# Layer 1's cross attention in a two-layer decoder: the value products turned round, and the softmax sums taken from the matrix unit to GpSimd and DRAM

## The chip, the cores and the metric

The kernel runs on one core of one Trainium2 chip. The core has five engines with queues of their own: TensorE (matrix products and transposes), VectorE, ScalarE, GpSimd and SyncE, which here only issues DMAs. The metric is the time of the whole program on the device in microseconds, as the median of several runs. In the profile the engines are called PE (matrix products), PEld (loading of the stationary operand), DVE (VectorE), ACT (ScalarE), POOL (GpSimd) and SP (SyncE); a trailing q marks an engine's queue, where DMAs are issued.

## The reference

Two decoder layers over x of 32 x 56 x 128, each with an attention over x or a recurrent mixer, a cross attention to a context of 32 x 1500 x 128, and a mixture of experts. All of it is fp32. The change touches only the cross attention of layer 1, which has 16 heads of 64:

```python
xn = _layernorm(x, ln_gamma, ln_beta)
q = (xn @ w_q).reshape(B, SQ, NUM_HEADS, DIM_HEAD)
k, v = jnp.split(context @ w_kv, 2, axis=-1)
k = k.reshape(B, SK, NUM_HEADS, DIM_HEAD)
v = v.reshape(B, SK, NUM_HEADS, DIM_HEAD)
scores = jnp.einsum('bqhd,bkhd->bhqk', q * SCALE, k)
attn = jax.nn.softmax(scores, axis=-1)
out = jnp.einsum('bhqk,bkhd->bqhd', attn, v).reshape(B, SQ, INNER)
out = (out @ w_out + b_out) * jnp.tanh(gate[0])
```

## The kernel before

The head matrices are folded at the start: key weights into the query projection (`m1`) and value weights into the output projection (`n1`). Each head's query then has 128 features and meets the raw context, so the attention of one batch element is 896 queries (16 heads x 56) against 1500 context rows of 128 features. Queries and, later, their results share the tiles `qo` (features on the partitions, queries along the row).

`attention()` takes the 896 queries of each of the 32 batch elements in two blocks of 512 and 384 (`BLOCKS`, line 66), 64 blocks in all. The 1500 context rows are 12 chunks of 125. For a block there are these steps:

- Scores (line 1088): 12 products, one a chunk, with a chunk of the transposed context `amT` stationary and the queries moving. The result has context rows on the partitions and queries along the row. ScalarE copies each from one of three PSUM banks (`p_s`) into the block's tile `s` (line 1089).
- Maxima: VectorE keeps a running elementwise maximum of the chunks in `m` (lines 1094 to 1098). TensorE transposes it, VectorE reduces it to the negative maximum of each query (`maxima`), and TensorE and ScalarE spread that over 125 partitions as `nb` (`spread`, line 1174).
- Probabilities (`probabilities`): in four parts of three chunks VectorE adds `nb` (line 1182) and ScalarE takes the exponential in place (line 1185).
- Values (`values`): for each 128 queries, 12 products with the probabilities stationary and the context rows `amN` moving, 129 columns wide; the last column of `amN` is one, so column 128 of the result is the sum of the probabilities. VectorE takes its reciprocal (line 1200), ScalarE scales by it into `ao` (line 1202).
- Outputs (`outputs`): TensorE transposes each `ao` (128 x 128) back, and VectorE copies the four or three of them into `qo` (line 1210).

The steps of three blocks are interleaved: while block i's scores are made, the rest of block i-1's probabilities (`tail`) and block i-2's outputs are done; then come block i-1's values, with block i's maxima and the first of its probabilities among them. The value results use two PSUM banks (`p_v`), the maxima's and outputs' transposes one (`p_t`), everything else two more (`p_f`).

Around this main thread run generators for everything that stands before layer 1's cross attention (`pre`, for four batch elements at a time) and behind it (`post`). Each `yield` of the attention is a place at which the loop at the end of `decoder_kernel` can let one of them go on; how far is decided by a planned time of TensorE (`clock["pe"]`), counted from the products issued, and by the constants `PRE_US`, `POST_US` and `PAIR_US`, the planned TensorE time of the attention of two batch elements. The framework's scheduler then fixes the order of instructions in each engine's queue. The layer norms take their inverse root on GpSimd (`root`, line 367, a power of one column), which is most of what GpSimd does. The big loads (`amT`, `amN`, expert weights) are issued from SP's queue.

Of the kernel before, what the change touches and what calls it, by code (L numbers as in the profile page):

```python
# [63 lines left out]
PRE_US, POST_US, PAIR_US = 71.3, 31.0, 80.5  # L64
# [5 lines left out]
def decoder_kernel(  # L70
# [88 lines left out]
    x_first = [const.tile([TP, D], F32, name=f"x_first{i}") for i in range(2)]  # L159
# [29 lines left out]

    qo = [const.tile([P, 2, NQ], F32, name=f"qo{i}") for i in range(3)]  # L190
# [878 lines left out]

    def attention():  # L1070
# [4 lines left out]
        for i in range(len(blocks) + 2):  # L1075
            cur = None
            if i < len(blocks):
# [8 lines left out]
                for c in range(CK):  # L1086
# [16 lines left out]
                    if c == 5 and old is not None:  # L1103
                        outputs(old)
                        old = None
# [4 lines left out]
            elif old is not None:  # L1110
                outputs(old)
                old = None
            for f in tail:
                f()
            tail = []
            os = []
            nt = prev[2] // P if prev else 0
            for t in range(max(nt, 2)):
                if t < nt:
                    po = values(prev, t)  # L1120
                    for k in range(3):
                        next(po)
                        if t == 1 and k == 1 and cur:
                            table["gelu"] = False
                            nb = spread(cur, nm)
                            tail = probabilities(cur, nb)
                            for f in tail[:1]:
                                f()
                            tail = tail[1:]
                        yield 0  # L1130
                    os.append(next(po))
                elif t == 1 and cur:
                    yield 1.0
                    nb = spread(cur, nm)
                    tail = probabilities(cur, nb)
                if t == 0 and cur:
                    if not nt:
                        yield 1.0
                    nm = maxima(cur, m)
                if t >= 2 and tail:  # L1140
                    tail.pop(0)()
            if prev:
                old = (prev, os)
# [45 lines left out]
    def values(blk, t):  # L1189
        b, _, _, s = blk  # L1190
        po = bank(p_v, "v")
        for c in range(CK):
            mm(
                po[:, : D + 1], s[:, c, t * P : (t + 1) * P], amN[b % 2][:, c, :],
                start=(c == 0), stop=(c == CK - 1),
            )
            if c % 4 == 3:
                yield
        rz = tiny.tile([P, 1], F32, tag="rz1", name="rz1")
        nc.vector.reciprocal(rz, po[:, D : D + 1])  # L1200
        o = work.tile([P, D], F32, tag="ao", name="ao", bufs=5)
        nc.scalar.activation(o, po[:, :D], AF.Copy, scale=rz)  # L1202
        yield o
# [203 lines left out]
```

## Time and profile before

| | |
|---|---|
| median of three runs | 2205.03 us (2204.17 to 2207.74) |
| the profiled execution, its own time | 2197.48 us |
| its span, first to last instruction | 2194.7 us |
| TensorE busy, granted clock | 2131.5 us (97%), 0.99 |
| VectorE busy | 1435.0 us (65%) |
| ScalarE busy | 1194.3 us (54%) |
| GpSimd busy | 143.8 us (7%) |
| DMA engines' mean share | 27.3% of 16 engines' time for the queue of the program's loads and stores |
| value products of layer 1 | 5376 instructions, 276 ns each from start to modelled end |
| scores of layer 1 | 768 instructions of 512 columns (594 ns) and 768 of 384 (493 ns) |
| transposes of `ao` | 224 instructions, 275 ns each |

A row of the profile reads: line, engine, operation, what is written and from what, the shapes, how many, and then times. Instructions of TensorE overlap, so a mean duration is longer than what one instruction adds; the start of one group and the start of the next tell what a group takes. An fp32 product appears as two instructions, a transpose as one. In the table of waits, the three numbers after a row are the total in us, how often, and the longest. In a timeline a row begins with the start and the length in us, and a bracket at its end gives the idle time in front of it and what ended that. A tile's own row gives the shortest, median and longest duration in ns.

### The profile page before, as it was taken

The page shows a single profiled execution, that of the slowest core. Times are in us where ns is not written, and L with a number is a line of the kernel's source. Part 1 is how long each engine was busy: PE and PEld are TensorE (multiplying, and loading weights), DVE is VectorE, ACT ScalarE, POOL GpSimd, SP SyncE. Part 2 cuts the span into 40 slices and gives each one's busy share as a digit, 9 for nine tenths or more (in the row PEclk, how much of TensorE's full clock was granted, in tenths as well). Part 3 has the DMA queues.
Part 4 walks back from the last instruction along what each step waited for, and adds up shares of the span by engine and source line. Part 5 has one row for each costly group of instructions (what it writes and reads, how often), then busy time and mean ns, then how long its engine had stood idle before and what let it go on. Part 6 is the DMA issues. An engine that isn't in the chain of part 4 may idle for free.

```text
span 2194.7 us, 36640 instructions
## 1 busy us (share of the span) xinstructions
PE 2131.5 (97%) x14496; PEld 1694.8 (77%) x14496; DVE 1435.0 (65%) x2961; ACT 1194.3 (54%) x2128; POOL 143.8 (7%) x230
## 2 busy tenths in 40 slices
PE   8899999999999999999999999999999999999997
PEld 5667787788777787777877788777887878778877
DVE  4377657765676756776577665777567765667774
ACT  3346655555654655555565656555555556465551
POOL 2010001000110001000010000100001000000000
PEclk8999999999999999999999999999999999999999
DMA  8503320153213432034311343113321132111221
GB/s 222 151 17 85 108 65 22 56 134 98 60 31 78 116 91 65 17 79 125 102 44 31 113 98 91 34 57 91 101 87 29 57 107 84 41 43 50 59 82 38
DMA packets 161996, 167.96 MB, mean 77 GB/s; under 512 B 9209, under 2 KB 136609, under 8 KB 161697
## 3 DMA queue, kind: packets, MB, share of 16 engines
q1 hardware_dynamic: 161568, 165.51, 27.3%
q8 instruction: 114, 1.87, 0.4%
q14 instruction: 58, 0.47, 0.1%
q10 hardware_dynamic: 256, 0.11, 0.0%
HBM read 140.09 MB, written 25.49 MB: 75 GB/s over the span
## 4 chain that ended last, share of the span: by engine, by line
PE 70%; DVE 9%; ACT 3%; POOL 2%; issue 1%; DMA 1%; POOLq 0%; DVEq 0%; ACTq 0%
PE f L146 25%; PE s L146 20%; PE v L146 19%; DVE s L1182 4%; PE f L155 3%; PE t L155 3%; POOL rs L367 2%; DVE m L1094 1%; ACT s L1185 1%; DVE m L1098 1%; ACT nb L1174 0%; DVE st L358 0%; DMA memT<-big 0%; DVE m L1096 0%; ACT s L1089 0%
## 5 line engine op out<-in xcount | busy, mean ns | idle before, releaser
L146 PE MATMUL v<-amN,s 125*128 125x129 f32 x5376 | 694.0, 276 | 0.0
L146 PEld LDWEIGHTS v<-amN,s 125*128 125x128 f32 x5376 | 655.0, 191 | 35.7 <-issue 23.3
L146 PE MATMUL s<-qo,amT 128*125 128x512 f32 (+1 forms) x1536 | 649.2, 543 | 1.6 <-ACT s L1089 1.5
L1089 ACT COPY s<-s 125x512 f32<-125x512 f32 (+1 forms) x768 | 399.7, 539 | 274.0 <-PE s L146 271.6
L1182 DVE TENSOR_TENSOR s<-s,nb 125x1536 f32<-125x1536 f32 (+1 forms) x256 | 393.0, 1547 | 61.2 <-ACT nb L1174 60.7
L146 PEld LDWEIGHTS s<-qo,amT 128*125 128x125 f32 x1536 | 263.4, 188 | 160.0 <-issue 95.3
L1185 ACT ACTIVATE s<-s 125x1536 f32<-125x1536 f32 (+1 forms) x256 | 339.5, 1330 | 86.4 <-DVE s L1182 81.0
L1094 DVE TENSOR_TENSOR m<-m,s 125x1024 f32<-125x1024 f32 (+1 forms) x192 | 209.1, 1089 | 67.3 <-ACT s L1089 64.7
L367 POOL TENSOR_TENSOR rs<-rs,mhalf 112x1 f32<-112x1 f32 x122 | 79.8, 664 | 1730.4 <-DVE rs L366 1559.0
L1202 ACT ACTIVATE ao<-v,rz 128x128 f32<-128x128 f32 x224 | 81.1, 363 | 164.4 <-DVE rz L1200 164.3
L772 ACT ACTIVATE hT<-f,vec 128x224 f32<-128x224 f32 x256 | 97.7, 447 | 89.8 <-PE f L146 89.5
L146 PEld LDWEIGHTS f<-wd,hT 128*112 128x112 f32 x1024 | 119.5, 177 | 19.2 <-ACT hT L772 8.8
L146 PE MATMUL f<-wd,hT 128*112 128x128 f32 x1024 | 128.8, 275 | 2.1 <-ACT hT L772 1.9
L146 PE MATMUL f<-pxT,w 128*128 128x224 f32 (+1 forms) x576 | 117.7, 344 | 2.5 <-DVE th L958 0.9
L146 PE MATMUL f<-xT,wu 128*128 128x224 f32 x512 | 114.7, 360 | 2.8 <-DMA wu<-in_wup_dram 2.7
L146 PEld LDWEIGHTS f<-pxT,w 128*128 128x128 f32 x576 | 99.0, 195 | 18.8 <-issue 3.5
L1094 DVE TENSOR_TENSOR m<-s 125x1024 f32<-125x1024 f32 x64 | 69.6, 1088 | 63.7 <-ACT s L1089 63.3
L146 PEld LDWEIGHTS f<-xT,wu 128*128 128x128 f32 x512 | 93.2, 192 | 19.9 <-issue 7.8
L790 DVE SCALAR_TENSOR_TENSOR acc<-f,wmix,acc 112x128 f32<-112x128 f32 x128 | 43.9, 348 | 88.8 <-PE f L146 88.7
L1098 DVE TENSOR_TENSOR m<-m,s 125x384 f32<-125x384 f32 (+1 forms) x128 | 80.4, 628 | 21.3 <-ACT s L1089 15.2
L1174 ACT COPY nb<-t 125x512 f32<-125x512 f32 x64 | 34.0, 531 | 103.7 <-PE t L155 103.7
L146 PE MATMUL f<-w,h 128*112 128x128 f32 x512 | 78.8, 276 | 2.4 <-DVE th L958 2.3
(302 smaller groups left out, 2321.1 us busy)
## 6 DMA issues: line engine op xcount, KB each, us to landing
amT<-memT SPq DMA_DIRECT2D x32, 750.0 KB
amN<-in_mem_dram SPq DMA_DIRECT2D x34, 672.0 KB
memT<-big SPq DMA_DIRECT2D x30, 750.0 KB
cxN<-in_mem_dram SPq DMA_DIRECT2D x30, 672.0 KB
wu<-in_wup_dram SPq DMA_DIRECT2D x64, 256.0 KB
wd<-in_wdn_dram SPq DMA_DIRECT2D x64, 256.0 KB
w<-in_gate_dram SPq DMA_DIRECT2D x72, 128.0 KB
w<-in_up_dram SPq DMA_DIRECT2D x72, 128.0 KB
```

The lines of the kernel that those rows point to most:

```text
L146: nc.tensor.matmul(ps, lhsT=lhsT, rhs=rhs, start=start, stop=stop)
L155: nc.tensor.transpose(ps, in_, ident[:k, :k])
L367: nc.gpsimd.tensor_tensor(rs, rs, mhalf[:TP], ALU.pow)
L772: nc.scalar.activation(hT[:, u0 + k, :], ps[:, k * nt : (k + 1) * nt], AF.Gelu, bias=vec[:, c : c + 1],)
L790: nc.vector.scalar_tensor_tensor(acc[j], down(last[1], last[0][1], nu, j), w[:, j, e - 1 : e], acc[j], ALU.mult, ALU.add,)
L1089: nc.scalar.copy(s[:, c, :], ps[:PK, :n])
L1094: nc.vector.tensor_tensor(m, a, s[:, c - 1 : c + 1, :], ALU.max)
L1098: nc.vector.tensor_tensor(m[:, 0, :], m[:, 0, :], s[:, c, :], ALU.max)
L1174: nc.scalar.copy(nb, ps[:PK, :n])
L1182: nc.vector.tensor_tensor(c, c, nb.unsqueeze(1).to_broadcast([PK, 3, n]), ALU.add)
L1185: nc.scalar.activation(c, c, AF.Exp)
L1202: nc.scalar.activation(o, po[:, :D], AF.Copy, scale=rz)
```

## The change

The value products have the context chunk stationary (`amN`, 128 columns, without the column of ones) and the probabilities of the whole block moving, 512 or 384 columns. One block is 12 products into one bank, with features on the partitions, as `qo` wants them, so the transposes of `outputs` go. The column of ones goes too, and the sums are made in another way:

- `chunk_sums`: five additions on GpSimd fold a block's 12 chunks in pairs into `zf` (125 x 2 x 512 or 384), issued during the scores of the next block.
- `inverse_sums`: TensorE sums `zf` over the partitions with a stationary tile of ones, 32 columns wide. The block's queries are cut into four quarters; each quarter's sum goes to one of four groups of 32 PSUM partitions, two products each. VectorE takes the reciprocal of the bank, 128 x 128 or 128 x 96.
- `store_sums` and `spread_sums`: a DMA from ScalarE's queue writes four partitions of this to a DRAM tile `zd`, and a second one reads it back to all 128 partitions as `rzb`, with the quarters in a row.
- `outputs`: VectorE multiplies the value bank by `rzb` into `qo`.

During the scores of block i, block i-2 has its reciprocal after the second score product, the store after the fifth, the load after the ninth and the multiplication after the twelfth. `rzb` shares its buffer with `nb`. The value bank is now held until that multiplication; a block's value bank is the one that the reciprocal of the block before has read. The maxima stand behind the third value product and the spread behind the fifth, instead of behind the first and the middle of the second group of 128 queries. `x_first`, the two first input tiles, lie in `qo`, which is not used yet then. `PAIR_US` is 78.1 instead of 80.5.

```diff
-PRE_US, POST_US, PAIR_US = 71.3, 31.0, 80.5
+PRE_US, POST_US, PAIR_US = 71.3, 31.0, 78.1
...
-    x_first = [const.tile([TP, D], F32, name=f"x_first{i}") for i in range(2)]
+    qo = [const.tile([P, 2, NQ], F32, name=f"qo{i}") for i in range(3)]
+    x_first = [qo[i][:TP, 0, :D] for i in range(2)]
...
+    ones = const.tile([PK, 32], F32, name="ones")
+    nc.gpsimd.memset(ones, 1.0)
...
+            adds = chunk_sums(prev) if prev else []
...
-                    if c == 5 and old is not None:
-                        outputs(old)
-                        old = None
+                    if adds and c in (2, 4, 6, 8, 10):
+                        adds.pop(0)()
+                    if old is not None:
+                        if c == 1:
+                            old = (*old, inverse_sums(old))
+                        elif c == 4:
+                            old = (*old, store_sums(old))
+                        elif c == 8:
+                            old = (*old, spread_sums(old))
+                        elif c == CK - 1:
+                            outputs(old)
+                            old = None
...
+            if prev:
+                po = bank(p_v, "v")
+            for c in range(CK):
+                if prev:
+                    value_chunk(prev, po, c)
+                if cur and c == 2:
+                    if not prev:
+                        yield 1.0
+                    nm = maxima(cur, m)
+                if cur and c == 4:
...
                     nb = spread(cur, nm)
                     tail = probabilities(cur, nb)
-                if t == 0 and cur:
-                    if not nt:
-                        yield 1.0
-                    nm = maxima(cur, m)
-                if t >= 2 and tail:
                     tail.pop(0)()
+                if tail and prev and (c == 8 or c == CK - 1 and prev[2] == 512):
+                    tail.pop(0)()
+                if prev:
+                    yield 0
...
-        nb = mid.tile([PK, 512], F32, tag="nb", name="nb")[:, :n]
+        nb = mid.tile([P, 512], F32, tag="nb", name="nb")[:PK, :n]
...
+    def chunk_sums(blk):
+        _, _, n, s = blk
+        f = mid.tile([P, 2, 512], F32, tag="zf", name="zf")[:PK, :, :n]
+
+        def add(c):
+            nc.gpsimd.tensor_tensor(
+                f, s[:, 0:2, :] if c == 2 else f, s[:, c : c + 2, :], ALU.add
+            )
+
+        sums[0] = f
+        return [lambda c=c: add(c) for c in range(2, CK, 2)]
+
+    def inverse_sums(old):
+        n, f = old[0][2] // 4, old[2]
+        ps = bank(p_v, "v")
+        for g in range(4):
+            for k in range(2):
+                mm(
+                    ps[32 * g : 32 * g + 32, :n], ones, f[:, k, g * n : (g + 1) * n],
+                    start=(k == 0), stop=(k == 1),
+                )
+        rz = work.tile([P, P], F32, tag="rz1", name="rz1", bufs=1)[:, :n]
+        nc.vector.reciprocal(rz, ps[:, :n])
+        return rz
+
+    def value_chunk(blk, po, c):
+        b, _, n, s = blk
+        mm(po[:, :n], amN[b % 2][:, c, :D], s[:, c, :], start=(c == 0), stop=(c == CK - 1))
+
+    def store_sums(old):
+        n = old[0][2] // 4
+        zd = dram.tile([4, P], F32, tag="zd", name="zd", bufs=4)[:, :n]
+        nc.scalar.dma_start(zd, old[3].rearrange("(g r) n -> g r n", g=4)[:, 0, :])
+        return zd
+
+    def spread_sums(old):
+        n = old[0][2]
+        rzb = mid.tile([P, 512], F32, tag="nb", name="rzb")[:, :n]
+        nc.scalar.dma_start(
+            rzb.rearrange("p (g n) -> p g n", g=4),
+            old[4].unsqueeze(0).to_broadcast([P, 4, n // 4]),
+        )
+        return rzb
...
-        (b, q0, n, _), os = old
-        ps = bank(p_t, "t")
-        for t, o in enumerate(os):
-            tr(ps[:, t * P : (t + 1) * P], o)
-        nc.vector.tensor_copy(qo[(b // 2) % 3][:, b % 2, q0 : q0 + n], ps[:, :n])
+        (b, q0, n, _), po, *_, rzb = old
+        nc.vector.tensor_tensor(
+            qo[(b // 2) % 3][:, b % 2, q0 : q0 + n], po[:, :n], rzb[:, :n], ALU.mult
+        )
```

More of the change, by code (lines that the diff above doesn't have):

```diff
@@ L188, in decoder_kernel @@
     memT = [dram.tile([P, CK * PK], F32, tag=f"memT{b}", name=f"memT{b}") for b in range(B)]
-    qo = [const.tile([P, 2, NQ], F32, name=f"qo{i}") for i in range(3)]
+    ones = const.tile([PK, 32], F32, name="ones")
+    nc.gpsimd.memset(ones, 1.0)
     qpad0 = const.tile([P, G, 64], F32, name="qpad")
@@ L1110, in attention @@
             elif old is not None:
-                outputs(old)
+                old = (*old, inverse_sums(old))
+                old = (*old, store_sums(old))
+                outputs((*old, spread_sums(old)))
                 old = None
-            for f in tail:
+            for f in tail + adds:
                 f()
             tail = []
[L1116 to L1132, printed above, removed]
-                    yield 1.0
+            if prev:
[8 more added lines that the diff above has]
+                if cur and c == 4:
+                    if not prev:
+                        yield 1.0
+                    table["gelu"] = False
                     nb = spread(cur, nm)
                     tail = probabilities(cur, nb)
-                if t == 0 and cur:
-                    if not nt:
-                        yield 1.0
-                    nm = maxima(cur, m)
-                if t >= 2 and tail:
                     tail.pop(0)()
+                if tail and prev and (c == 8 or c == CK - 1 and prev[2] == 512):
+                    tail.pop(0)()
+                if prev:
+                    yield 0
             if prev:
-                old = (prev, os)
+                old = (prev, po, sums[0])
             if cur and cur[1] == 0 and cur[0] + 1 < B:
@@ L1187, in probabilities @@
         return [lambda k=k: part(k) for k in range(4)]
[L1189 to L1195, printed above, removed]
-            )
[L1197 to L1203, printed above, removed]
@@ new lines, in decoder_kernel @@
+    sums = [None]
+    def inverse_sums(old):
[13 more added lines that the diff above has]
+        mm(po[:, :n], amN[b % 2][:, c, :D], s[:, c, :], start=(c == 0), stop=(c == CK - 1))
```

## The prediction

> **What bounds the kernel now.** I read the page's busy times first.
>
> ```profile
> span 2194.7 us, 36640 instructions
> PE 2131.5 (97%) x14496; PEld 1694.8 (77%) x14496; DVE 1435.0 (65%) x2961; ACT 1194.3 (54%) x2128; POOL 143.8 (7%) x230
> ```
>
> TensorE is busy for 97% of the span, and in the page's 40 slices it is at eight tenths or more in all but the last, at the full clock, so there is no stage in which another engine takes over. So a change is worth what it takes from TensorE's order of instructions, less the waits it puts there. Busy time counts overlapping groups twice, so I took costs from TensorE's timeline, as the time from one group's start to the next group's start:
>
> ```profile
> 1014.43 5.53 PE L146 MATMUL v<-amN,s 125*128 125x129 f32 x48
> 1019.79 0.60 PE L146 MATMUL f<-w,h 128*112 128x128 f32 x4
> ...
> 1021.32 1.89 PE L146 MATMUL s<-qo,amT 128*125 128x512 f32 x4
> 1023.05 0.60 PE L146 MATMUL f<-w,h 128*112 128x128 f32 x4
> ```
>
> Each fp32 product is two instructions here. A value instruction costs (1019.79 - 1014.43)/48 = 112 ns for 129 moving columns, a score instruction (1023.05 - 1021.32)/4 = 432 ns for 512. Summed over the whole trace: 5376 value instructions take 640.7 us, 13.5 of it idle at their ends; the scores take 433 ns each at 512 columns and 340 at 384; the 224 transposes of `ao` take 26.7 us.
>
> **The change on TensorE.** (a) Values: per batch element 84 products of 129 columns become 12 of 512 and 12 of 384, over 32 elements 768 instructions of each width. At the scores' price that is 768 x 433 + 768 x 340 = 594 us, 47 less. The new products stay in one bank and wait for no score copy; two score instructions in an undisturbed run take 0.85 and 0.65 us, which gives 576 us, 65 less. I take the middle, **-55**.
>
> (b) The `ao` transposes go: **-27**. With them goes this wait (the waits of TensorE):
>
> ```profile
> PE t L155 <- DVE rz L1200: 6.4, 5, 1.7
> ```
>
> **-6**. The 224 reciprocals and 224 scalings on VectorE and ScalarE were beside TensorE and are worth nothing else.
>
> (c) Added: eight products a block with `ones`, 16 instructions in four column groups of 32. The nearest row is the mask product of layer 0, also 16 instructions of 32 columns by 128:
>
> ```profile
> 386.13 0.64 PE L146 MATMUL f<-big,vmask 112*32 112x128 f32 x16
> 386.59 0.58 PE L146 MATMUL f<-big,hT 112*32 112x56 f32 x32
> 387.10 0.59 PE L146 MATMUL s<-qo,amT 128*125 128x384 f32 x1
> ```
>
> It takes 0.46 us where one after the other would take 16 x 0.107, so all four groups run at once; returning to the full array costs some 0.14 more (0.51 for the `hT` run against 32 x 0.047 / 4 = 0.37). That is 0.60 us a block of 512 and 0.49 for 384: 64 x 0.55 = **+35**. But `vmask` walks the groups with the inner loop, and `inverse_sums` puts both products of a group one behind the other, four instructions. If a group's four hold back the next group until the last of them, 13 turns of 0.107 or 0.080 us plus 0.14 are 1.36 us a block, +87. I take the row; +35 to +87 is the bound.
>
> (d) New waits on TensorE. In the built program's order the first value product of a block stands directly behind the sums of the block before in seven cases (under 2 us of work between), and it takes the bank that the reciprocal reads. That reciprocal is now 128 columns on all partitions; the row of layer 0 says 0.85 us for 112:
>
> ```profile
> L551 DVE RECIPROCAL o<-f x15: 848/851/859, 20.9 to 1716.1; 128x112 f32<-128x112 f32 x15
> ```
>
> 0.14 + 0.97 and 0.7 for VectorE's queue against 0.7 to 1.9 us of cover: **+4** (0 to 10). Elsewhere 3 to 22 us of TensorE work lie between.
>
> (e) The end: the last block has no scores to hide behind. Before, `qo` was written 1.8 us after the last value product. Now: sums 0.6, reciprocal 0.75, store, load, product 0.6, and five additions ending about 1 us late. For a load the trace starts at 0.8 us with two DMAs on ScalarE's queue that landed by 2.98 (2.2 us), and a broadcast of 260 KB, nearly the new load's 256 KB:
>
> ```profile
> 1.72 0.44 SPq L172 DMA_DIRECT2D row<-in_rows_dram  x1
> 5.54 0.20 ACT L278 ACTIVATE tgate<-row 128x1 f32<-128x1 f32 x1 [2.53 <-DMA row<-in_rows_dram]
> ```
>
> So 3.4 us from the end of issue, at the busiest time of all. With 2.6 for the store and 3.3 for the load the end comes **+7** later (5 to 10).
>
> **The change elsewhere.** ScalarE loses 81 us and issues 128 DMAs at 0.44 us, 56 us; the load waits in its queue for the store, and score copies stand behind it. The program has 2.0 to 4.5 us of TensorE work between store and load, the trip needs 2.6; three score banks hide 0.87 us each. **+3** (0 to 25). VectorE: reciprocals 64 x 0.85 - 36 = +18 us of busy time, the final product as long as the copy of before; nothing on the path. SP's queue is untouched. `ones` is one memset more ahead of `qpad` in POOL's queue, hidden behind the first load (2.98). `x_first` in `qo` costs nothing: `qo` is first written after 100 us. PAIR_US changes when side work is offered, not its amount.
>
> GpSimd gets 320 additions of 125 x 1024 or 768. Its nearest rows are 0.445 us for 112 x 128 and this (`kb`, 448 columns):
>
> ```profile
> L471 POOL TENSOR_TENSOR kb<-kT,hmask x15: 922/1281/1377, 8.8 to 1689.6; 128x448 f32<-128x448 f32 x15
> ```
>
> A slope of 1.5 ns a column and 0.25 us: 1.8 and 1.4 us, 8 us a block. The Trainium skill (GPSIMD Engine Reference, section 3.1) gives 4497 ns for 2048 columns, so an estimate of 2.35 and 1.8, 10.3 us a block. I take the trace; both fit into a block's 34 us, and the sums are consumed a whole value phase later. What counts is who is held up meanwhile:
>
> ```profile
> 1016.69 1.35 DVE L1182 TENSOR_TENSOR s<-s,nb 125x1152 f32<-125x1152 f32 x1
> 1016.85 1.59 POOL L367 TENSOR_TENSOR rs<-rs,mhalf 112x1 f32<-112x1 f32 x1 [79.10 <-DVE rs L366]
> ...
> 1018.48 0.34 DVE L372 TENSOR_SCALAR y<-r,mv,rs 112x128 f32<-112x128 f32 x1 [0.35 <-POOL rs L367]
> ```
>
> A power of one column, 0.55 us as a median, took 1.59 because it ended 0.4 us after VectorE's product of two SBUF operands. The skill (SBUF — State Buffer, "Who interferes with whom") says why: VectorE's second SBUF input and GpSimd share a port, exclusively for the whole instruction. The trace shows GpSimd losing; the rule also lets VectorE lose, and speaks against this change. Without it the additions cost TensorE nothing. With it, in the stretch from a block's first score to its maxima (19 stretches measured):
>
> ```profile
> 854.64:873.42 18.78, 18.06 (x95) 12.23 (x93) 15.58 (x36) 13.39 (x24) 3.15 (x5) 1.00 0.32 82
> ...
> sum 434.81, PE 428.52 PEld 308.17 DVE 278.66 ACT 247.74 POOL 22.79; mean PE 22.55 PEld 16.22 DVE 14.67 ACT 13.04 POOL 1.20
> ```
>
> (window, length, then PE, PEld, DVE, ACT, POOL.) VectorE is busy 14.7 of 22.9 us there, some 8 of them with two SBUF inputs (maxima 6.2, additions of `nb` 2.0). Each of five additions meets one with a chance of 0.4 and holds it some 1 us: 2 us a block, 128 us of VectorE in all, over an idle third. The powers of layer norm also stand behind additions in POOL's queue, and VectorE waits for them in its own: 56 groups, perhaps one in six late by 3 us, 28 us. Bounds on TensorE: 0 if the idle third takes all, 156 if nothing does. Long stretches absorb it, those of 18 us (15.6 busy) do not: **+20**.
>
> **Sum**: -55 - 27 - 6 + 35 + 4 + 7 + 3 + 20 = -19. The profiled execution took 2197.5 us (span 2194.7 and 2.8 around it), so 2178.5; the median of the runs stands 7.5 above that execution: **2186 us**. A measurement tells 0.2% (4.4 us) from no change.
>
> **The rivals.** *Slower, by GpSimd*: in the short stretches VectorE becomes the bound, the maxima come late, and their transposes stand two or three value products after the scores, so TensorE waits there. Without the GpSimd term the sum is -39, 0.6 us a block; beyond that the change loses. At 1.5 us a block, 96 instead of 20: 2262 us. For it: 15.6 of 18.8 us busy. Against: maxima had 1.2 us of value products as cover and now have 2 to 2.6. *The column groups don't overlap*: +52, 2238 us. For: the order of the loops; against: the mask row. *The round trip is late*: the final product stands among the maxima in VectorE's queue, 2.4 to 4 us of work after the load's issue, which needs 3.3 to 3.8. One microsecond late a block, half of it reaching TensorE: +32, 2218 us. *Everything hidden*: (a) at -65, no term for GpSimd, ScalarE or the reciprocal: 2186 - 37 = 2149 us.
>
> **How the numbers follow.** Forecast (2165 to 2205) 0.42, of it 0.40 faster and 0.02 same; everything hidden 0.12, faster; column groups 0.10, 0.03 same and 0.07 slower; GpSimd 0.28 (2205 to 2290), 0.02 same and 0.26 slower; round trip 0.08: 0.01, 0.02, 0.05. Together faster 0.53, same 0.09, slower 0.38. The range 2150 to 2250 leaves out a twentieth below and half of GpSimd's case above. The forecast's own range is 2165 to 2205.
>
> **What would show it.** Value instructions at 425 to 433 and 325 to 340 ns; 16 `zf` instructions in 0.6 us (over 1 us: the groups don't overlap); additions of 1.4 to 2.4 us; in the waits, TensorE for `m` at its transposes (GpSimd's rival), ScalarE or VectorE for a DMA of `zd` or `rzb` (round trip). I am wrong if TensorE's idle time grows from 63 us to over 100.

## The result, and the profile after

The changed kernel takes 2520.8 us (median; 2514.0 to 2525.9) against 2204.6 for the one before: 1.1437 times as long, 95% interval 1.1420 to 1.1454. The forecast was 2186 us, its range ended at 2250. The profile of after, first its busy times and the row of TensorE's granted clock:

```profile
span 2520.5 us, 30966 instructions
...
PE 2239.7 (89%) x11456; PEld 1414.5 (56%) x11456; DVE 1752.2 (70%) x2801; ACT 1133.8 (45%) x1902; POOL 918.2 (36%) x551
...
PEclk9899999999999998899989999799997999899998
```

TensorE has 3040 instructions fewer and is busy for longer. Its idle time, span less busy time, has gone from 63 to 281 us; the prediction named 100 as the mark at which it would be wrong. What TensorE waits for (us in total, times, longest):

```profile
PE t L155 <- DVE m L1105: 61.5, 21, 5.6
PE f L146 <- DVE big L851: 25.1, 4, 8.7
PE f L155 <- DVE h L375: 19.6, 10, 5.9
PE f L155 <- DVE th L961: 14.8, 3, 4.9
```

All are waits for VectorE: the maxima (`m`), but also the side work, where three or four waits sum up to 15 or 25 us. For the same 2801 instructions VectorE is busy 295 us longer than in the kernel without the additions (1752.2 against 1456.8 us, next section). Its groups (count, busy us, mean ns, then the idle time before them):

```profile
L1101 DVE TENSOR_TENSOR m<-m,s 125x768 f32<-125x768 f32 x96 | 188.6, 1965 | 23.8 <-ACT s L1096 22.0
L1101 DVE TENSOR_TENSOR m<-m,s 125x1024 f32<-125x1024 f32 x96 | 154.4, 1608 | 20.0 <-ACT s L1096 17.9
...
L793 DVE SCALAR_TENSOR_TENSOR acc<-f,wmix,acc 112x128 f32<-112x128 f32 x128 | 43.6, 346 | 80.5 <-PE f L146 80.3
...
L819 DVE SCALAR_TENSOR_TENSOR xT<-hp,vec,xT 128x224 f32<-128x224 f32 x14 | 14.2, 1014 | 0.3
```

The same groups before (L819 was line 816):

```profile
L1094 DVE TENSOR_TENSOR m<-m,s 125x768 f32<-125x768 f32 x96 | 92.0, 958 | 30.2 <-ACT s L1089 27.8
L1094 DVE TENSOR_TENSOR m<-m,s 125x1024 f32<-125x1024 f32 x96 | 117.2, 1221 | 37.1 <-ACT s L1089 37.0
...
L816 DVE SCALAR_TENSOR_TENSOR xT<-hp,vec,xT 128x224 f32<-128x224 f32 x14 | 6.3, 448 | 0.3
```

The means mix two cases. In the changed kernel 31 of the 96 maxima of 768 columns meet no addition and take 966 ns on average; the 65 that do take 2441. L793 takes what it always took (348 ns before): one of its operands comes from PSUM. On GpSimd:

```profile
L1206 POOL TENSOR_TENSOR zf<-zf,s 125x1024 f32<-125x1024 f32 x128 | 355.0, 2774 | 9.7
L1206 POOL TENSOR_TENSOR zf<-zf,s 125x768 f32<-125x768 f32 x128 | 275.6, 2153 | 10.0
```

With the two groups of first additions they take 771 us, where the prediction had 512. One place shows how the two engines meet (start, duration, engine, instruction; in brackets the idle time ahead of it and its releaser):

```profile
663.04 11.06 POOL L1206 TENSOR_TENSOR zf<-zf,s 125x1024 f32<-125x1024 f32 x4
...
664.50 2.42 DVE L815 TENSOR_SCALAR xT<-hp,vec 128x224 f32<-128x224 f32 x1
...
666.96 4.94 DVE L819 SCALAR_TENSOR_TENSOR xT<-hp,vec,xT 128x224 f32<-128x224 f32 x2
671.82 3.10 DVE L1101 TENSOR_TENSOR m<-s 125x768 f32<-125x768 f32 x1
...
671.95 1.33 PE L146 MATMUL f<-xT,sq 128*32 128x224 f32 x3 [7.13 <-DVE xT L819]
```

Four additions run one behind another. Each VectorE instruction that meets them stands for about one addition, whatever its own length: 2.4 us each, three in a row. TensorE waits 7.1 us at the end of this chain. The same place in windows of 5 us (busy time and count of PE, PEld, DVE, ACT, POOL; then the granted clock, the DMA share and GB/s):

```profile
660.00:665.00 5.00, 4.31 (x11) 1.66 (x10) 5.00 (x4) 3.71 (x7) 4.33 (x2) 1.00 0.61 146
665.00:670.00 5.00, 0.00 (x0) 0.00 (x0) 4.93 (x3) 1.52 (x2) 4.84 (x3) 0.87 0.00 0
670.00:675.00 5.00, 3.05 (x6) 1.35 (x7) 5.00 (x3) 0.88 (x2) 4.02 (x2) 0.50 0.00 0
```

From 665 to 670 VectorE and GpSimd are both "busy" all the time with three instructions each. After the stall TensorE works at half clock: 0.50 in the third window. The Trainium skill (TensorE: Matmul & The Clock Gate, "Part 1: The HAM clock gate") has the clock halved after an idle stretch of some 3.4 us, and this stretch of 7 fits. So a stall is paid twice, and busy time grows with idle time: 2239.7 against 2128.2 us for the same instructions without additions (next section), at a mean clock of 0.94 against 0.99. Summed over TensorE's busy time, what the granted clock withheld is 116 us here and 18 there, so 98 of these 112 us are the clock's.

One step of the prediction came out as written, the sums with `ones`:

```profile
1226.79 1.88 PE L146 MATMUL s<-qo,amT 128*125 128x512 f32 x4
1228.60 0.66 PE L146 MATMUL v<-zf,ones 125*32 125x128 f32 x16
1229.19 1.78 PE L146 MATMUL f<-xT,wu 128*128 128x224 f32 x8
```

Sixteen instructions in 0.6 us: the column groups do run at once with both products of a group one behind the other.

### The profile page after: what moved, and what is told of

Read it like the earlier page. It is cut to its first block, busy times and chain, and to the rows that moved or that the text cites. A ratio compares the mean times of both kernels' runs of the same rounds, so it can differ in the third digit from the quotient of the medians.

```text
span 2520.5 us, 30966 instructions
## 1 busy us (share of the span) xinstructions
PE 2239.7 (89%) x11456; PEld 1414.5 (56%) x11456; DVE 1752.2 (70%) x2801; ACT 1133.8 (45%) x1902; POOL 918.2 (36%) x551
## 4 chain that ended last, share of the span: by engine, by line
PE 56%; DVE 27%; POOL 6%; issue 5%; ACT 4%; DMA 2%; ACTq 0%; SPq 0%; DVEq 0%; POOLq 0%
PE f L146 21%; PE v L146 18%; PE s L146 11%; DVE m L1101 11%; DVE s L1194 4%; POOL zf L1206 4%; PE f L155 3%; PE t L155 2%; POOL rs L370 2%; DVE m L1105 2%; ACT s L1096 1%; DMA rzb<-zd 1%; ACT s L1197 1%; DVE m L1103 1%; ACT hT L775 1%
## 5 line engine op out<-in xcount | busy, mean ns | idle before, releaser
L146 PE MATMUL v<-s,amN 125*128 125x512 f32 (+1 forms) x1536 | 688.8, 567 | 3.7 <-DVE rz L1225 2.0
L146 PE MATMUL s<-qo,amT 128*125 128x512 f32 (+1 forms) x1536 | 671.1, 558 | 5.4 <-ACT s L1096 5.4
L1206 POOL TENSOR_TENSOR zf<-zf,s 125x1024 f32<-125x1024 f32 (+1 forms) x256 | 630.6, 2463 | 19.7
L1206 POOL TENSOR_TENSOR zf<-s 125x1024 f32<-125x1024 f32 x64 | 140.7, 2198 | 963.1 <-PE v L146 772.9
L1194 DVE TENSOR_TENSOR s<-s,nb 125x1536 f32<-125x1536 f32 (+1 forms) x256 | 406.3, 1606 | 78.3 <-ACT nb L1186 78.0
L146 PEld LDWEIGHTS s<-qo,amT 128*125 128x125 f32 x1536 | 275.8, 193 | 191.1 <-issue 114.2
L1101 DVE TENSOR_TENSOR m<-m,s 125x1024 f32<-125x1024 f32 (+1 forms) x192 | 343.0, 1787 | 43.7 <-ACT s L1096 39.9
L146 PEld LDWEIGHTS v<-s,amN 125*128 125x128 f32 x1536 | 280.0, 199 | 166.4 <-issue 102.3
L1101 DVE TENSOR_TENSOR m<-s 125x1024 f32<-125x1024 f32 x64 | 127.5, 1993 | 42.8 <-ACT s L1096 42.5
L155 PE MATMUL t<-ident,m 125*128 125x125 f32 x224 | 42.4, 308 | 65.0 <-DVE m L1105 61.5
L793 DVE SCALAR_TENSOR_TENSOR acc<-f,wmix,acc 112x128 f32<-112x128 f32 x128 | 43.6, 346 | 80.5 <-PE f L146 80.3
```

Source lines behind the costliest of these rows:

```text
L146: nc.tensor.matmul(ps, lhsT=lhsT, rhs=rhs, start=start, stop=stop)
L155: nc.tensor.transpose(ps, in_, ident[:k, :k])
L793: nc.vector.scalar_tensor_tensor(acc[j], down(last[1], last[0][1], nu, j), w[:, j, e - 1 : e], acc[j], ALU.mult, ALU.add,)
L1101: nc.vector.tensor_tensor(m, a, s[:, c - 1 : c + 1, :], ALU.max)
L1194: nc.vector.tensor_tensor(c, c, nb.unsqueeze(1).to_broadcast([PK, 3, n]), ALU.add)
L1206: nc.gpsimd.tensor_tensor(f, s[:, 0:2, :] if c == 2 else f, s[:, c : c + 2, :], ALU.add)
```

## The experiments

**Theory**: the additions on GpSimd hold VectorE through the shared port, and all 320 us come from there. **Rivals**: GpSimd's queue (powers and other side work late behind additions), the round trip by way of DRAM, the new order of the value products itself. The four first kernels ran on a chip on which the kernel before took 2202.5 us.

**Without the additions.** `zf` is a constant of ones, so the kernel leaves the softmax's own sums out; all else stays.

```
-        f = mid.tile([P, 2, 512], F32, tag="zf", name="zf")[:PK, :, :n]
-
-        def add(c):
-            nc.gpsimd.tensor_tensor(
-                f, s[:, 0:2, :] if c == 2 else f, s[:, c : c + 2, :], ALU.add
-            )
-
-        sums[0] = f
-        return [lambda c=c: add(c) for c in range(2, CK, 2)]
+        sums[0] = zfix[:PK, :, :n]
+        return []
```

> The changed kernel without the 320 additions on GpSimd: the sums are taken from a constant tile of ones, so the probabilities' sums are left out and all else stays (products with ones, reciprocal, store, load, final product). My theory, that the additions hold up VectorE and that all of the loss is theirs: near the sum of the prediction without its GpSimd term, 2166 us, 2140 to 2190, with a granted clock back at 0.99. Rival, the round trip by way of DRAM, or the later maxima: still over 2300. Rival, the clock falls because of the longer matrix products: the clock stays near 0.94 and the time over 2250.

2200.4 us, ratio 0.9993 (0.9983 to 1.0002). The busy times of this kernel:

```profile
PE 2128.2 (97%) x11456; PEld 1365.5 (62%) x11456; DVE 1456.8 (66%) x2801; ACT 1131.0 (51%) x1902; POOL 141.1 (6%) x232
```

The additions are the whole loss of 320 us. But the gain that the sum had without them, 39 us, isn't there either. I return to that below.

**The kernel before, with the additions alone.** Their result is used by nothing; for want of memory each is cut in two halves of the columns, which share one buffer, and `x_first` lies in `qo`, as after.

```
+            adds = chunk_sums(prev) if prev else []
...
+                    if adds and c in (2, 4, 6, 8, 10):
+                        adds.pop(0)()
```

> The kernel before with the additions on GpSimd alone, in the same places, their result not used; each of them cut in two halves of columns because less memory is free. My theory: they alone make it 250 to 400 us slower, about 2500 us, and the clock falls to 0.93 to 0.95. Rival, that it takes the new value products or the round trip as well: under 2260.

2443.8 us (one run), 241 more than before. The additions do it in either kernel; the value products in their new order are not needed for it.

**Memsets in place of the additions.** Each addition becomes three memsets of `zf`, so GpSimd is busy as long (946 us) and its queue as full; the sums are left out.

```
-            nc.gpsimd.tensor_tensor(
-                f, s[:, 0:2, :] if c == 2 else f, s[:, c : c + 2, :], ALU.add
-            )
+            for _ in range(REP):
+                nc.gpsimd.memset(f, 1.0)
```

> The changed kernel with each addition replaced by three memsets of the same tile on GpSimd, so GpSimd is busy about as long (600 to 850 us) and its queue stands before the powers of layer norm in the same way, but nothing is read from SBUF; the probabilities' sums are left out. Theory of the shared port: VectorE is not held by instructions that only write, so the maxima take 0.95 and 1.22 us again and the time is 2150 to 2230. Rival, GpSimd's queue in front of the powers: 2400 to 2550, with VectorE waiting for GpSimd.

2227.0 us (one run): 27 of the 320. The groups of VectorE and GpSimd in this kernel:

```profile
L1102 DVE TENSOR_TENSOR m<-m,s 125x768 f32<-125x768 f32 x96 | 91.7, 955 | 33.3 <-ACT s L1097 31.7 <-DVE pacc L981 0.2
...
L1208 POOL MEMSET zf<- 125x1024 f32 x480 | 457.2, 952 | 572.6 <-PE v L147 549.2
```

The maxima are at 955 ns (957 without additions) beside a GpSimd that only writes, although 89 of these 96 meet a memset. So what holds instructions with two SBUF inputs is GpSimd's reading, and the queue is a small thing here: all of it is within the 27 us. Writing is not harmless, though. Instructions with one input, from SBUF to SBUF, are held by memsets too, as here in the layer norm (first without additions, then beside memsets; a mean of 368 and of 705 ns):

```profile
L377 DVE TENSOR_SCALAR y<-r,mv,rs 112x128 f32<-112x128 f32 x45 | 16.3, 368 | 13.6 <-POOL rs L372 13.4
L376 DVE TENSOR_SCALAR y<-r,mv,rs 112x128 f32<-112x128 f32 x45 | 28.7, 705 | 13.7 <-POOL rs L371 13.6
```

**The same additions on VectorE**, one word changed, nothing left out.

```
-            nc.gpsimd.tensor_tensor(
+            nc.vector.tensor_tensor(
                 f, s[:, 0:2, :] if c == 2 else f, s[:, c : c + 2, :], ALU.add
```

> The changed kernel with the same additions on VectorE instead of GpSimd; it computes everything. VectorE gets 320 x 1.1 us = 345 us more work without anything being held twice. Theory of the shared port: no addition costs more than its own 1.2 or 0.95 us, VectorE is at some 80%, and the time is 2190 to 2290. Rival, that the sums come too late or VectorE's load is all that counts: over 2400.

2211.3 us, ratio 1.0043 (1.0026 to 1.0059): 310 us faster than on GpSimd, and 11 slower than with no additions at all. The engine that was meant to be relieved does them in half the time and in gaps:

```profile
L1206 DVE TENSOR_TENSOR zf<-zf,s 125x1024 f32<-125x1024 f32 x128 | 155.4, 1214 | 0.8
...
L1101 DVE TENSOR_TENSOR m<-m,s 125x768 f32<-125x768 f32 x96 | 90.8, 946 | 1.3 <-ACT s L1096 1.0
```

The idle time of VectorE ahead of these maxima, in which it waited for a score copy, was 35.4 us without additions and is 1.3 here.

**No round trip.** The kernel without additions, without the store and the load too; the final product takes a constant.

```
-        nc.scalar.dma_start(zd, old[3].rearrange("(g r) n -> g r n", g=4)[:, 0, :])
-        return zd
+        return None
...
-        nc.scalar.dma_start(
-            rzb.rearrange("p (g n) -> p g n", g=4),
-            old[4].unsqueeze(0).to_broadcast([P, 4, n // 4]),
-        )
-        return rzb
+        return zfix[:, 0, :n]
```

> The kernel without the additions, and without the store and the load of the reciprocals too (the final product takes a constant in their place; the sums and the reciprocal are still computed, of constants). Without the additions it took 2200.4 us. My theory: the round trip is hidden everywhere but at the end, where TensorE waits 4.2 us for qo and the rest is the time of flight, so 2193 us, 7 less. Rival (the trip was what ate the gain on TensorE that I had counted on): 2170 us or less.

2186.1 us, ratio 0.9921 (0.9908 to 0.9935) against 0.9993 with the trip: it costs 0.72%, 16 us, more than the 7 of either the expectation or the end alone. In the timelines of TensorE the two kernels differ by 7 us at the end (`qo`) and by 5 around the value products of 512 columns.

**The additions issued later**, behind value products 1, 3, 5, 7 and 9, and the sums two scores later.

```
-                    if adds and c in (2, 4, 6, 8, 10):
-                        adds.pop(0)()
...
+                if adds and c in (1, 3, 5, 7, 9):
+                    adds.pop(0)()
```

> The changed kernel with the five additions on GpSimd moved out of the score phase into the value phase (behind value products 1, 3, 5, 7 and 9), so that they meet the additions of the maxima to the scores and the side work, but only the first maxima of the next block; the sums are taken two scores later. My theory (what an addition meets on VectorE with the shared port decides, and the side work's chains are met anywhere): some of the loss stays, 2350 to 2450 us. Rival (the loss is the maxima alone, because only they have a deadline): 2210 to 2260. Rival (the number of additions decides, not their place): 2500 to 2540.

2600.8 us, ratio 1.1799 (1.1782 to 1.1815): outside all three expectations, and slower than the change. The edit didn't do what I meant. GpSimd runs its queue as soon as operands and buffers allow; the first addition waits for `zf` to be read by the sums of the block before (TensorE's products end 823 us of GpSimd's waiting for its additions), not for a value product. So the additions still ran in the score phase, two scores later: some 620 of their 792 us lie between a block's first and last score product, 679 of 771 in the changed kernel (the maxima of 768 columns took 2099 ns, of 1024 1787).

**One addition of five**, the others left out of the sum: `range(2, 4, 2)` in place of `range(2, CK, 2)`.

> The changed kernel with only the first of the five additions of a block (so four fifths of the sum are left out). Without additions it took 2200 us and with all five 2521. If every addition costs the same (no slack takes them up), 64 us for one: 2264 us. If VectorE's idle third absorbs a part, as my prediction had it, and the loss begins only beyond it: 2200 to 2220.

2213.9 us, ratio 1.0045 (1.0030 to 1.0060), 14 us more than none (11 by the spans, and by the ratios; the two were measured on different chips). The second of the two theories holds for the first addition. In a stretch that I followed it ends before the first maximum begins, and over the whole run that maximum keeps its time (986 ns for 768 columns, 958 without additions); what it holds is an addition of `nb` (1833 ns on average in place of 1746), before the next chunk of probabilities.

**The maxima's transposes two value products later**, on the kernel with the additions on VectorE; the spreading moves by two as well, and one later part of the probabilities by one.

```
-                if cur and c == 2:
+                if cur and c == 4:
...
-                if cur and c == 4:
+                if cur and c == 6:
```

> The kernel with the additions on VectorE (2211.3 us) with the transposes of the maxima two value products later (behind the fifth in place of the third), the spreading of the maxima two later too. If the idle time at the ends of the runs of value products (some 14 us without additions, waits for m of 6 to 12 us) is what was missing from the gain of the value products: 2203 us, 8 less. If the later probabilities cost as much at the other end: 2211 us or more.

2211.4 us, ratio 1.0034 (1.0021 to 1.0048): no change. TensorE's wait for `m` falls from 6.4 to 4.0 us and nothing comes of it.

**No maxima.** The changed kernel with one maximum over the first and the last chunk in place of ten over all (a smaller number in the exponent; the quotient stays what it was).

```
-                    if c % 2 == 1 and 1 < c < CK - 2:
...
-                    elif c >= CK - 2:
-                        nc.vector.tensor_tensor(m[:, 0, :], m[:, 0, :], s[:, c, :], ALU.max)
+                    if c == CK - 1:
+                        nc.vector.tensor_tensor(m[:, 0, :], s[:, 0, :], s[:, c, :], ALU.max)
```

> The changed kernel with the maxima over a block's chunks left out but for one over the first and the last chunk (a smaller number is taken from the exponent, the quotient is the same). VectorE loses some 9 of the 10 products of two SBUF operands in a score phase, all that the additions are seen to hold there with a deadline on TensorE. If the maxima are where the 320 us are lost: 2200 to 2250 us. If the side work's chains (layer norm, expert products), held by the same port, lose as much on their own: 2350 us and more.

2330.7 us, ratio 1.0585 (1.0566 to 1.0604), between the two expectations: with one maximum a block left, the additions still cost some 130 us. VectorE's instructions grow by 112 us there, 100 of them in the side work and 12 in the additions of `nb`.

**Three additions of five**: `range(2, 8, 2)`.

> The changed kernel with three of the five additions of a block (two fifths of the sum left out). None: 2200 us, one: 2214, five: 2521. If the port fills up (what is asked of it by the score phase's maxima and by the additions, one after the other, against the length of the phase), the first ones are nearly free and the last dear: 2270 to 2330. If every one after the first costs the same: 2367. If only the very last counts (the sums come late): below 2240.

2340.3 us, ratio 1.0625 (1.0606 to 1.0643), between the first two theories. None, one, three and five additions give 2200, 2214, 2340 and 2521 us: 14 us for the first, 63 for each of the next two, 90 for each of the last two. Number and place change together in this row, since the additions left out are always the last.

**The round trip on SP's queue**, on the kernel with the additions on VectorE: `nc.sync.dma_start` for both.

> The kernel with the additions on VectorE (2211.3 us), its store and load of the reciprocals issued on SP's queue in place of ScalarE's. If what the round trip costs besides the end is ScalarE standing in its queue behind a DMA's wait: 2203 to 2207. If it is something else: 2210 to 2212.

2211.2 us, ratio 1.0043 (1.0029 to 1.0057): no change. ScalarE's queue isn't what the trip costs.

**The additions really in the value phase.** Ahead of the first addition GpSimd copies one column of the next block's negated maxima into `zf`, which the addition then overwrites.

```
                     nm = maxima(cur, m)
+                    if prev:
+                        nc.gpsimd.tensor_copy(sums[0][:, 0, 0:1], nm[:PK, 0:1])
...
+                if adds and c in (3, 4, 5, 6, 7):
+                    adds.pop(0)()
```

> The changed kernel with the additions really in the value phase: a copy of one column of the next block's negated maxima, ahead of the first addition on GpSimd and overwritten by it, lets them begin only when the maxima are done (in the kernel with the additions only issued later, they still began as soon as the buffer of the sums came free, in the score phase). Sums, store and load come three, two and one score later than in the changed kernel. If the maxima are what must not be held, and the additions to the scores can be late: 2230 to 2350 us. If the additions only have to overlap with VectorE's work, whichever: 2480 us and more.

2664.9 us, ratio 1.2111 (1.2089 to 1.2133), the slowest of all and in the range of the second theory. The additions did move (606 of their 877 us lie between a block's first and last value product, 219 of 771 in the changed kernel), and what VectorE suffers has moved with them:

```profile
L1196 DVE TENSOR_TENSOR s<-s,nb 125x1152 f32<-125x1152 f32 x128 | 338.2, 2655 | 29.6 <-ACT nb L1188 26.7 <-POOL zf L1208 2.8
L1196 DVE TENSOR_TENSOR s<-s,nb 125x1536 f32<-125x1536 f32 x128 | 333.7, 2631 | 23.2 <-ACT nb L1188 23.1
L1101 DVE TENSOR_TENSOR m<-m,s 125x1024 f32<-125x1024 f32 x96 | 117.2, 1221 | 27.2 <-ACT s L1096 26.7
L1101 DVE TENSOR_TENSOR m<-m,s 125x768 f32<-125x768 f32 x96 | 91.6, 954 | 33.5 <-ACT s L1096 32.2
```

The maxima are at their old durations (1221 and 957 ns without additions), and the additions of `nb`, 1348 and 1864 ns in the changed kernel, take 2655 and 2631. On top of it the sums come late, and TensorE waits for GpSimd itself:

```profile
PE v L146 <- POOL zf L1208: 71.6, 10, 10.7
```

**The additions cut into quarters.** This run and the next ask what was still open: why VectorE's idle third takes up so little.

```
-            nc.gpsimd.tensor_tensor(
-                f, s[:, 0:2, :] if c == 2 else f, s[:, c : c + 2, :], ALU.add
-            )
+            q = n // 4
+            for lo in range(0, n, q):
+                cut = slice(lo, lo + q)
+                nc.gpsimd.tensor_tensor(
+                    f[:, :, cut], s[:, 0:2, cut] if c == 2 else f[:, :, cut],
+                    s[:, c : c + 2, cut], ALU.add,
+                )
```

> The changed kernel with every addition on GpSimd cut into four of a quarter of the columns (1280 in place of 320, the same sums). In the runs so far the time lost stands close to the time by which VectorE's instructions grew: 295 us grown and 320 lost in the changed kernel, 156 and 140 with three additions, 23 and 14 with one. Cutting tells why they grow. If an instruction of VectorE stands until the addition that runs has ended (2.4 or 1.8 us alone, a quarter 0.7 or 0.5), growth and loss shrink with the length of one: 2300 to 2370 us. If the port is given out by the time that is asked of it, so that the sum counts and not the length: 2480 us or more.

2475.5 us, ratio 1.1239 (1.1206 to 1.1271), just under what the second theory asked for, 45 us less than uncut. Yet the growth of VectorE's instructions did shrink with the length of one addition, from 295 to 163 us; the first theory is right there. The rest came by another road: a block's twenty additions last longer (1024 us in all, against 771). Most of that is the cost of having more instructions. At their shortest a quarter takes 0.71 or 0.58 us and a whole addition 2.33 or 1.80, which comes to 824 us in place of 661. The other 90 us are time in which additions were held up; that VectorE gets its turn between the pieces is my reading. The powers of layer norm stand behind the additions:

```profile
1005.20 14.49 POOL L1209 TENSOR_TENSOR zf<-zf,s 125x256 f32<-125x256 f32 x16
...
1019.65 0.55 POOL L370 TENSOR_TENSOR rs<-rs,mhalf 112x1 f32<-112x1 f32 x1
1020.23 0.35 DVE L375 TENSOR_SCALAR y<-r,mv,rs 112x128 f32<-112x128 f32 x1 [5.68 <-POOL rs L370]
...
1021.17 0.89 PE L155 MATMUL t<-ident,m 125*128 125x125 f32 x3 [6.22 <-DVE rs L369]
```

A power that was ready at 1013.7 (VectorE's `rs`) runs at 1019.65. VectorE waits for it in order, with the last maximum behind it in its queue, and TensorE waits 6.2 us for that.

**One addition in two scores.** A copy of one column into a tile `gate`, ahead of every addition on GpSimd, waits for a score copy.

```
+                        nc.gpsimd.tensor_copy(gate, s[:, c, 0:1])
                         adds.pop(0)()
```

> The changed kernel with every one of the five additions held back by a copy of one column on GpSimd that waits for a score copy (third, fifth, seventh, ninth and eleventh of the next block), so that the additions don't run in one burst but one in two scores. If the burst is what hurts (five additions behind one another leave VectorE no turn without one): 2300 to 2400 us. If every addition that meets VectorE costs what it holds, wherever: 2480 to 2560 us.

2527.7 us, ratio 1.1471 (1.1446 to 1.1496), as the changed kernel. But the gates held back little: 0.6 us each on average (193 us over 315 copies), since two scores take less time than one addition. So this run doesn't rule the burst out.

**The runs side by side.** For each kernel I take two numbers from the profile of VectorE. "Grown" is its busy time less that of the kernel without additions (1456.8 us; for the kernel before with additions, 1435.0). "Waiting" is the sum of all its waits for GpSimd, less that of the same base (50.8; 56.3). "Lost" is the span less that of the base (2198.4; 2194.7). For the run without maxima both busy times are those of all other instructions (1204.0 against 1092.0 us); a span for that base wasn't measured.

| kernel | grown | waiting | together | lost |
|---|---|---|---|---|
| one addition | 24 | 1 | 25 | 11 |
| memsets | 20 | 8 | 28 | 27 |
| three additions | 157 | 7 | 164 | 141 |
| no maxima | 112 | 52 | 164 | 131 |
| quarters | 163 | 95 | 258 | 268 |
| before, with additions | 216 | 63 | 279 | 247 |
| changed kernel | 295 | 22 | 317 | 322 |
| one in two scores | 299 | 24 | 323 | 332 |
| issued later | 342 | 30 | 372 | 402 |
| really in the value phase | 335 | 44 | 379 | 464 |

From three additions on, every microsecond by which GpSimd holds VectorE up costs the kernel 0.8 to 1.2 (the 464 hold 72 of TensorE waiting for GpSimd itself). Two things stand in "lost", though. In the changed kernel TensorE's idle time is 211 us more (281 against 70), two thirds of the 317, and its busy time 112 more, most of it the clock's; in the other rows from three additions on the idle time is 0.55 to 0.85 of "together". So VectorE's slack did take up a part, and the clock put back about as much: that 317 and 322 are so close is a coincidence of the two. Against it stands the kernel with the additions on VectorE: 285 us of busy time more, and 12 us of span.

## Why the prediction was wrong

**The GpSimd term is the step that failed**: "Bounds on TensorE: 0 if the idle third takes all, 156 if nothing does. Long stretches absorb it [...]: +20". It measured +320. The sign and the mechanism (VectorE held while an addition runs) stand in the prediction; the sizes of the term did not fit. Three were off, and one part, the clock, was put at nothing:

- *The additions themselves.* Undisturbed they take 2.35 and 1.81 us (the first additions in the kernel with the gate), not the 1.8 and 1.4 of the slope between the rows of 128 and 448 columns. The estimate from the figure of the Trainium skill (GPSIMD Engine Reference, section 3.1), weighed there and left aside, was 2.35 and 1.8 (its working isn't shown; in plain proportion 4497 ns for 2048 columns is 2.25 and 1.69). A straight line was no mistake: at their shortest, additions of 192, 256, 768 and 1024 columns take 0.58, 0.71, 1.80 and 2.33 us in these runs, 2.1 ns a column and 0.17 us, which gives 0.44 for 128 columns, as the prediction's first row says. It is `kb`, at its shortest 0.92 us for 448 columns where this line has 1.12, that was no row for them. It multiplies by a mask of a few columns that is repeated by a broadcast; whether that makes it shorter was not tested.
- *How much VectorE is held.* 2 us a block and 28 us of powers made 156 us. It was 317: 22 of waiting for the powers, about as expected, and 295, 4.6 us a block, of held instructions. The maxima alone give 191 (470 against 279 us), 3.0 a block. Missing in the prediction is the side work that reads SBUF only, one-input forms among them (L815 above, 2.42 us), each standing as long as an addition runs.
- *How much of it reaches TensorE.* I took 20 of 156, an eighth. It was two thirds (211 of 317 us, as TensorE's idle time), and with the clock, for which the prediction has no term, as much as was held. This is the largest of the three: with the whole of my own 156 us the sum would have been 2322. Idle time as a mean over a stage doesn't say that a delay fits into it. As I read the timelines, the held instructions stand in chains, TensorE to VectorE and back, that are short of time just then, and the idle time lies where VectorE waits for score copies; no run separates the two.

Why the same work on VectorE costs so little is not shown by a run. I read it thus: in VectorE's own queue an addition of 1.2 us fills a gap ahead of a maximum (35.4 us of waiting became 1.3), and delays what follows by that at most; on GpSimd five of 2.4 us run without regard to what VectorE needs next. The quarters support the part on length and met a new wait instead. The burst stays open.

**Rivals.** The rival "slower, by GpSimd" named mechanism, place and sign (waits for `m` at its transposes, the maxima late), at 96 us and a chance of 0.28. It too lacked the side chains and the clock: TensorE's waits for `m` are 61.5 of its 281 us of idle time. The column groups (+52) and a late round trip as the cause of it all are out.

**The other steps**, read from the kernel without additions by the time from one group's start to the next, as in the prediction:

- *(a) values, -55*: 608.5 against 640.7, -32. The price was right: without idle time 594.8, the 594 of the scores' price. But 13.5 us of idle time at the ends were in the 640.7 and not in the 594, and 6 of these were taken off again in (b). They came back as 13.7: the wait for the reciprocals of before went, and the wait for the maxima rose:

```profile
PE t L155 <- DVE m L1107: 12.0, 12, 2.5
PE f L146 <- DVE qo L1244: 4.2, 1, 4.2
```

- *(b) transposes of `ao`, -27*: gone, as said. *The wait, -6*: counted twice, see (a).
- *(c) sums, +35*: 25.1 + 15.9 = 41. Right in kind; the ends of a group cost a little more.
- *(d) the reciprocal, +4*: TensorE's wait for `rz` is 2.0 us. Right.
- *(e) the end, +7*: the products that read `qo` take 66.6 in place of 58.2 us over the whole run, and 59.2 without the trip; the difference lies in the last 32 of them, 10.2 us with the trip and 4.2 without. Right.
- *ScalarE and DMAs, +3*: the scores take 8.9 us more, and the trip costs 16 with the end, against 10 in the sum. That it is not ScalarE's queue is shown; what it is stays open.

Values 23 and the wait 6 worse, the sums 6, the scores 6 above the 3 that I had, a few us of side work: the 39 us are used up, and the timelines differ by +4 us. So the change would have been level without its additions, not faster; with them on VectorE it is level to half a per cent slower. No version here beats the kernel before while it computes everything.

## What to carry to other kernels

Before work is moved to an idle GpSimd, list every VectorE instruction that it will overlap and that touches SBUF alone; price each as standing for one whole GpSimd instruction, and take the sum as lost unless the chain behind it is seen to have time (here the first of five additions was nearly free, the others were not). Where the stalls are long, add the clock. Compare with leaving the work on VectorE: there it took half as long, and the order in the queue put it into gaps. And when two totals are compared, both hold idle time or neither does.

## What was not expected of the hardware

The runs show three cases. Instructions with a PSUM operand aren't held (L793 346 ns). Those with two SBUF inputs are held by additions, which read (958 to 1965 ns), and not by memsets, which only write (955 ns). And one-input instructions from SBUF to SBUF are held by both (L815 2.42 us beside additions, the layer norm's `y` 705 ns in place of 368 beside memsets). The Trainium skill (SBUF — State Buffer, "Who interferes with whom") has the same three, the last for forms that use both of VectorE's ports. Unexpected was how little it takes: GpSimd at 36% busy made the kernel 14% slower, and moving the additions from one phase to the other moved the harm with them, the maxima back at 1221 and 954 ns. Cutting an instruction on the shared port into four lengthens the work as a whole (1024 us for 771), some two thirds of it by the cost of more instructions alone.
